# First image's product by channel block while loading, tables copied by ScalarE, second tables and early loads spread over the last image

## Chip, core and metric

The kernel runs on one core of a Trainium2 chip. The metric is device time in microseconds, from one launch to its end. The engines are named as in the profile: PE is TensorE (its weight loads are shown apart as PEld), DVE is VectorE, ACT is ScalarE, POOL is GpSimd, SP is SyncE, which here only issues DMAs. DMAs are issued from SP, ACT and POOL.

## What is computed

The input is a batch of 4 images with 256 channels of 56 x 56 in float32. Four layers follow, each adding its result to its input after a group norm (32 groups of 8 channels):

```
x = x + involution_0(gn(x))     # a 7x7 kernel for each pixel and each of 16 groups of channels
x = x + resblock_1(gn(x))       # two 3x3 convolutions with batch norm, relu, residual
x = x + involution_2(gn(x))     # as layer 0, with batch norms and relu
x = x + gates_3(gn(x))          # a channel gate and a spatial gate

# involution:
h    = reduce_w @ x + reduce_b            # 256 -> 64 channels, at each pixel
kern = span_w @ h + span_b                # 64 -> 16 groups x 49 taps, at each pixel
out[group, c, y, x] = sum over taps of kern[group, tap, y, x] * x[c, y + dy, x + dx]
```

## The kernel before

**Data.** An image is held as two blocks of 128 channels, `[128, 3136]` each. The function `new_block` hands out one of three such buffers. A *unit* is one block of one image, so a layer has eight units. Layers pass images on through DRAM.

**An involution layer** (`involution_layer`, layers 0 and 2). The 56 x 56 pixels are cut into tiles of 3 x 8 (`TY`, `TX`), 19 rows of tiles by 7 columns. `bottleneck` makes `h` for one image: it scales the reducing weights by the norm's factor (L404), multiplies them with the image (L433, at most 9 rows of pixels in one matmul, two row groups side by side in the two halves of the PSUM partitions), evicts with ACT (L450) and copies each half to the other half of the partitions with DVE (L441). The result `hp` is one buffer (`new_h`).

For each unit `tap_matrices` then runs 32 steps. A step multiplies a shifted window of the span weights, `z_sb`, with `hp` (L471) and adds the biases `zb_sb` while evicting: three steps in four by DVE (L489), one by ACT (L482). The result `kt` holds, for each tile, a matrix that takes the 14 x 9 pixels around the tile to the tile's 24 pixels. After each step the functions in `hooks[step]` are called; that is how other work gets its place in the order.

Then come the unit's seven columns of tiles (`apply`): PE multiplies windows `xw` of the image with `kt` (L513), ACT and DVE pick the wanted quarter of each product (L526, L533), and in layer 0 POOL adds it to the image (L538). The windows of a column are made three columns ahead (`NXW`): `next_strip` normalises a strip of the image (POOL, L364), `next_windows` transposes it on PE (L381), ACT copies it out (L382), and four DMAs on SP and POOL shift parts of it within SBUF (L388, L390). Work in `late[column]` follows a column, work in `early[column]` comes before it. `column_sums` takes the statistics for the next layer's norm, and `norm_steps` is a chain of single operations across DVE, PE and POOL that ends in rstd and shift.

**Tables.** `make_tables` builds `z_sb` and `zb_sb` from the span weights: it loads them, copies 16 pieces of 49 elements (L300), two pieces of the biases (L308), makes 24 small matmuls (48 records, L315) and copies the result (L322), with DVE for all copies. In layer 0 it is called once for this layer and once for layer 2; the second result is kept in DRAM until layer 2 begins. The second call is placed in the first unit at steps 3, 14 and 21, and saved at step 22.

**The opening** of layer 0 (L732 to 738): the statistics and norms of both blocks, `bottleneck(0)`, the first tables, `batch_norms`. `since = mark()` comes after these lines (L750): what is written before it is ordered by the planner that places instructions, with its own costs; what follows up to `in_order(since)` keeps on each engine the order in which it is written.

**The convolution layer** (`conv_layer`) transforms rows of the image into six positions (Winograd in the columns, `transform`, L1047 and on) and multiplies them (L1131, L1160, L1242) with weights that were transformed by `row_weights` (L964 to 971). Its first input rows and its first raw weights are loaded ahead by `begin_conv`, which the last unit of layer 0 calls after its first column (`late[0]`, L847). `phases` normalises the rows and sorts them by the four positions; for the first rows ACT does block 0 and DVE block 1 (L1037, L1039). `row_weights` issues its loads from ACT (L952, L953). All eight of these DMAs, four per convolution, carry 384 KB.

Of the kernel before, what the change touches and what calls it, by code (L numbers as in the profile page):

```python
# [16 lines left out]
P = 128  # L17
# [48 lines left out]
def run(g):  # L66
    for _ in g:
        pass
# [3 lines left out]
def net_kernel(  # L72
# [68 lines left out]
    def bn_fold(name, par, gamma, beta, mean, var, n):  # L141

        s = const.tile([P, n], F32, name=f"{name}_s")
        t = const.tile([P, n], F32, name=f"{name}_t")
        rsqrt_eps(s, par(var), BN_EPS)
        nc.vector.tensor_mul(s, s, par(gamma))
        nc.vector.tensor_mul(t, par(mean), s)
        nc.vector.tensor_sub(t, par(beta), t)
        return s, t

# [8 lines left out]
    def batch_norms():  # L159

        par_of = {}
# [8 lines left out]
        s1, t1 = bn_fold("bn1", by_channel, L1_G1, L1_B1, L1_M1, L1_V1, NB)  # L170
        s2, t2 = bn_fold("bn2", by_channel, L1_G2, L1_B2, L1_M2, L1_V2, NB)
        s4, t4 = bn_fold("bn4", by_channel, L2_G, L2_B, L2_M, L2_V, NB)
        s3, t3 = bn_fold("bn3", by_row, L2_G1, L2_B1, L2_M1, L2_V1, 1)

        s4_of = {}
        for n in (2, 4):
            s4_of[n] = const.tile([P, n, NB], F32, name=f"s4_{n}")
            for i in range(n):
                nc.vector.tensor_scalar_mul(s4_of[n][:, i, :], s4, par_of[n][:, i : i + 1])
        bn.update(par=par_of, s1=s1, t1=t1, s2=s2, t2=t2, s3=s3, t3=t3, s4=s4_of, t4=t4)  # L180
# [55 lines left out]
    def load_block(dst, block, parts=1):  # L236
        n = NCHUNK // parts
        for j in range(0, NCHUNK, n):
            at = slice(j * CR * W, min(j + n, NCHUNK) * CR * W)
            nc.sync.dma_start(dst[:, at], block[:, at])  # L240

    def involution_layer(layer, xin, xout, red, span, sb, xs_of, ahead=None, pending=None):

        with ExitStack() as es:
# [12 lines left out]
            def warm(n):  # L257

                ps = one_bank()
                for _ in range(n):  # L260
                    nc.tensor.matmul(ps[:, :P], ident_sb, ident_sb, start=True, stop=True)

            def load(b, cb, parts=1):
                xs_of[b, cb] = new_block()
                load_block(xs_of[b, cb], xin[b][cb], parts)

            for cb in range(NB):
                if (0, cb) not in xs_of:
                    load(0, cb, 3)

            red_sb = wpool.tile([P, NB, 2, R], F32, name="red_sb")
            for i in range(2):
                nc.scalar.dma_start(red_sb[:, :, i], red.rearrange("(cb p) r -> p cb r", p=P))
# [3 lines left out]
            def make_tables(z_sb, zb_sb, span, sb, scratch, eng):  # L277
# [8 lines left out]
                bias_f = scratch[:, n + KK * KK : n + KK * KK + ZN]  # L286
                for i in range(2):
# [4 lines left out]
                nc.gpsimd.memset(z_sb, 0.0)  # L292
                nc.gpsimd.memset(bias_f, 0.0)
                yield
                for i in range(2):
                    half = slice(i * R, (i + 1) * R)
                    for cb in range(NB):
                        m = GB // 2
                        for gp in range(m):
                            nc.vector.tensor_copy(  # L300
                                field(z_sb[half, cb * m + gp, :]),
                                taps[half, cb, :, 2 * gp + i].rearrange("p (y x) -> p y x", x=KK),
                            )


                for i in range(2):
                    half = slice(i * R, i * R + G)
                    nc.vector.tensor_copy(field(bias_f[half]), bias_g[half])  # L308
                yield
                pair = two_banks()  # L310
                for p in range(TP):
                    k, i = divmod(p, 2)
                    half = slice(i * R, i * R + G)
                    z0 = ZF - p // TX * QX - p % TX
                    nc.tensor.matmul(  # L315
                        pair[:Q, i, k * G : (k + 1) * G],
                        bias_f[half, z0 : z0 + Q],
                        ident_sb[half, half],
                        start=True,
                        stop=True,  # L320
                    )
                nc.vector.tensor_copy(  # L322
# [1145 lines left out]
```

## Time and profile before

| | |
|---|---|
| median of 3 runs | 1877.03 us (1874.28 to 1877.57) |
| the profiled execution | 1874.37 us, its span 1872.6 us |
| mean granted PE clock | 0.966 |
| busy share | PE 91%, PEld 81%, DVE 77%, ACT 40%, POOL 23% |
| opening, to the first tap matrix | 36.6 us |
| first unit: tap matrices, columns | 36.0 us, 32.2 us |
| third unit: tap matrices, columns | 24.0 us, 30.3 us |
| last unit of layer 0: tap matrices, columns | 24.0 us, 42.6 us |
| from layer 0's last matmul to the convolution's first | 18 us |

The profile is that of one execution. A line such as `L471 PE MATMUL ps<-hp,z_sb 64*126 64x133 f32` names the line of the kernel, the engine, the operation, and its output and inputs; a matmul in float32 leaves two records. "Busy" is time with an instruction in the engine. A wait names the engine that ended it. The chain of waits follows the work that ended last backwards. SPq, ACTq and POOLq are the queues from which DMAs are issued. In the answers in order of time the columns are start, time, engine, line, operation, and in brackets how long the engine had been idle and what ended that.

### The profile page before, as it was taken

The page shows a single profiled execution, that of the slowest core. Times are in us where ns is not written, and L with a number is a line of the kernel's source. Part 1 is how long each engine was busy: PE and PEld are TensorE (multiplying, and loading weights), DVE is VectorE, ACT ScalarE, POOL GpSimd, SP SyncE. Part 2 cuts the span into 40 slices and gives each one's busy share as a digit, 9 for nine tenths or more (in the row PEclk, how much of TensorE's full clock was granted, in tenths as well). Part 3 has the DMA queues.
Part 4 walks back from the last instruction along what each step waited for, and adds up shares of the span by engine and source line. Part 5 has one row for each costly group of instructions (what it writes and reads, how often), then busy time and mean ns, then how long its engine had stood idle before and what let it go on. Part 6 is the DMA issues. An engine that isn't in the chain of part 4 may idle for free.

```text
span 1872.6 us, 55573 instructions
## 1 busy us (share of the span) xinstructions
PE 1709.5 (91%) x24030; PEld 1509.6 (81%) x24030; DVE 1433.3 (77%) x2823; ACT 748.8 (40%) x1657; POOL 432.2 (23%) x615
## 2 busy tenths in 40 slices
PE   5999999999759999999999999997999898898866
PEld 3888888888748988898899889885877777778865
DVE  5687777876678988898888988865767777777763
ACT  2445445454423222232223212114666565565532
POOL 2323433244210000000000000000000581681672
PEclk9999999999979999999999999998999999999995
DMA  3445544453533111110111210223533764773652
GB/s 97 150 146 177 153 120 140 152 153 111 160 121 100 42 60 61 61 67 36 62 58 57 73 35 33 89 76 89 174 107 132 231 193 147 222 215 105 177 147 76
DMA packets 65589, 215.72 MB, mean 115 GB/s; under 512 B 13564, under 2 KB 20528, under 8 KB 61504
## 3 DMA queue, kind: packets, MB, share of 16 engines
q1 hardware_dynamic: 44448, 141.62, 24.1%
q0 software_dynamic: 14848, 65.85, 10.9%
q10 hardware_dynamic: 6048, 4.68, 0.8%
q8 instruction: 190, 3.11, 0.7%
q14 instruction: 55, 0.45, 0.1%
HBM read 76.24 MB, written 49.16 MB: 67 GB/s over the span
## 4 chain that ended last, share of the span: by engine, by line
PE 65%; DVE 21%; DMA 5%; POOL 3%; issue 3%; ACT 2%; SPq 1%; POOLq 0%; ACTq 0%; DVEq 0%
PE mm L1242 20%; PE ps L513 14%; DVE kt L489 12%; PE mm L1160 10%; PE ps L471 7%; PE mm L1131 6%; PE ps L381 4%; DMA xw<-xw 3%; PE ps L433 2%; DVE un L533 2%; PE ps L700 1%; ACT hp L452 1%; PE ps L596 1%; DVE st L844 1%; DMA xs<-in_x_dram 1%
## 5 line engine op out<-in xcount | busy, mean ns | idle before, releaser
L513 PE MATMUL ps<-kt,xw 126*32 126x48 f32 (+1 forms) x12544 | 383.5, 236 | 56.9 <-DMA xw<-xw 21.3
L513 PEld LDWEIGHTS ps<-kt,xw 126*32 126x32 f32 (+1 forms) x12544 | 344.2, 122 | 102.4 <-issue 48.1
L471 PE MATMUL ps<-hp,z_sb 64*126 64x133 f32 x6144 | 389.0, 282 | 19.2 <-DVE kt L489 7.0
L471 PEld LDWEIGHTS ps<-hp,z_sb 64*126 64x126 f32 x6144 | 370.7, 189 | 34.1 <-DVE kt L489 8.7
L489 DVE TENSOR_TENSOR kt<-ps,zb_sb 126x798 f32<-126x798 f32 x384 | 357.9, 978 | 43.6 <-PE ps L471 43.1
L1242 PE MATMUL mm<-v,u_sb 128*128 128x280 f32 (+1 forms) x1728 | 384.9, 384 | 3.3 <-DVE v L1067 3.3
L1242 PEld LDWEIGHTS mm<-v,u_sb 128*128 128x128 f32 x1728 | 327.6, 190 | 57.8 <-DVE v L1067 3.6
L482 ACT ACTIVATE kt<-ps,zb_sb 126x133 f32<-126x133 f32 x768 | 224.0, 441 | 179.4 <-PE ps L471 179.4
L1160 PE MATMUL mm<-v,u_sb 128*128 128x252 f32 (+1 forms) x936 | 211.2, 386 | 12.6 <-DVE v L1051 12.6
L1160 PEld LDWEIGHTS mm<-v,u_sb 128*128 128x128 f32 x936 | 177.2, 190 | 42.9 <-issue 12.6
L533 DVE SCALAR_TENSOR_TENSOR un<-ps,par_sb,un 128x240 f32<-128x240 f32 x224 | 98.4, 457 | 103.1 <-ACT un L526 98.8
L533 DVE SCALAR_TENSOR_TENSOR un<-ps,s,un 128x240 f32<-128x240 f32 x224 | 102.3, 457 | 92.9 <-ACT un L528 88.7
L1279 POOL DMA_DIRECT2D x<-xs x24 | 13.1, 546 | 684.9 <-DVE xs L1278 539.5
L1227 ACT ACTIVATE res<-xs,shift,norm_sb 128x1120 f32<-128x1120 f32 (+1 forms) x24 | 30.2, 1260 | 235.2 <-DVE xs L1278 119.7
L538 POOL TENSOR_TENSOR xs<-un,xs 128x240 f32<-128x240 f32 x112 | 72.4, 665 | 224.2 <-DVE un L533 224.1
L382 ACT COPY xw<-ps 126x896 f32<-126x896 f32 x112 | 101.5, 907 | 49.6 <-PE ps L381 39.2
L381 PE MATMUL ps<-ident_sb,strip_sb 128*126 128x128 f32 x784 | 111.4, 282 | 1.6 <-DVE kt L489 0.8
L526 ACT ACTIVATE un<-ps,par_sb 128x240 f32<-128x240 f32 x112 | 50.1, 448 | 138.6 <-PE ps L513 136.7
L1131 PE MATMUL mm<-xs,u_sb 128*128 128x126 f32 (+1 forms) x792 | 98.3, 277 | 1.3 <-DVE xs L1094 1.0
L528 ACT ACTIVATE un<-ps,bn_t,s 128x240 f32<-128x240 f32 x112 | 60.1, 538 | 97.8 <-PE ps L513 93.7
L139 POOL TENSOR_TENSOR norm_sb<-norm_sb,mhalf 128x1 f32<-128x1 f32 x32 | 19.2, 602 | 341.7 <-DVE norm_sb L138 341.7
L1131 PEld LDWEIGHTS mm<-xs,u_sb 128*128 128x128 f32 x792 | 94.3, 191 | 2.7 <-issue 1.4
(194 smaller groups left out, 1973.0 us busy)
## 6 DMA issues: line engine op xcount, KB each, us to landing
xw<-xw SPq DMA_DIRECT2D x168, 252.0 KB
xw<-xw SPq DMA_DIRECT2D x224, 126.0 KB
xw<-xw POOLq DMA_DIRECT2D x56, 252.0 KB, 4.7
xs<-x SPq DMA_DIRECT2D x24, 560.0 KB
x<-xs POOLq DMA_DIRECT2D x8, 1568.0 KB, 7.9
xs<-x SPq DMA_DIRECT2D x8, 1568.0 KB
xs<-in_x_dram SPq DMA_DIRECT2D x6, 1568.0 KB
x<-xs SPq DMA_DIRECT2D x6, 1568.0 KB
```

The lines of the kernel that those rows point to most:

```text
L381: nc.tensor.transpose(ps[:Q, k * P : (k + 1) * P], flat[:, k * Q : (k + 1) * Q], ident_sb)
L382: nc.scalar.copy(xw[:, :NSB, :], ps[:Q, : NSB * P].rearrange("q (n c) -> q n c", n=NSB))
L471: nc.tensor.matmul(ps[:Q, i, k * NT : (k + 1) * NT], z_sb[i * R : (i + 1) * R, cb * GB // 2 + gp, z0 : z0 + Q], hp[i * R : (i + 1) * R, py ...
L482: nc.scalar.activation(kt[:, g0 + i, pb, :, k], ps[:Q, i, k * NT : (k + 1) * NT], AF.Identity, bias=zb_sb[:, cb * GB + g0 + i, p0 + k : p0 ...
L489: nc.vector.tensor_tensor(kt[:, g0 : g0 + 2, pb], ps[:Q, :, : PB * NT].rearrange("q i (k t) -> q i t k", k=PB), zb_sb[:, cb * GB + g0 : cb ...
L513: nc.tensor.matmul(v[m * j : m * j + m, i, :, k * TP : (k + 1) * TP], xw[:, window(ty), m * j : m * j + m], kt[:, ng * j : ng * j + ng, :, ...
L528: nc.scalar.activation(part, o[0], AF.Identity, bias=bn["t4"][:, cb : cb + 1], scale=bn["s4"][ng][:, 0, cb : cb + 1])
L533: nc.vector.scalar_tensor_tensor(part, o[e], s, part, ALU.mult, ALU.add)
L538: nc.gpsimd.tensor_tensor(dst, u, dst, ALU.add)
L1131: nc.tensor.matmul(ps[:, co * m : (co + 1) * m], u[ci][:, co * P : (co + 1) * P], v2[:, e, : n // 2, ci * WT : (ci + 1) * WT], start=(ci = ...
L1160: nc.tensor.matmul(ps, u1_sb[:, ci, dy, k, co * P : (co + 1) * P], v[:, k, dy * NB + ci : (dy + n - 1) * NB + ci + 1 : NB, :], start=(j == 0),
L1242: nc.tensor.matmul(ps, u2_sb[:, ci, dy, k, co * P : (co + 1) * P], v[:, k, dy * NB + ci : (dy + n - 1) * NB + ci + 1 : NB, :], start=(j == 0),
```

## The change

In layer 0:

- The first image is loaded in pieces of 4 and 3 chunks (a chunk is eight rows) for block 0 and of 2, 2, 2, 1 for block 1, all from SP. ACT makes one small copy at once. Everything from here on keeps the written order.
- A new function `begin` holds the whole opening. It issues the loads for the first tables and the reducing weights from POOL. The first image's product is no longer made by `bottleneck`: full-width matmuls for block 0 come as soon as its norm is there, and those for block 1 after the second norm. The weights are in both halves, so the copies between the halves are gone. Evictions alternate between ACT and DVE.
- `make_tables` copies with ACT instead of DVE, and yields after every piece; its 24 matmuls can be made in several parts.
- The second tables move from the first unit to the last image: loads at step 16 of the seventh unit, three pieces after each of six of its columns (the last of these is the first of six parts of the matmuls), the other five parts at steps 3 to 18 of the eighth unit, saved at step 22.
- `batch_norms` is a generator whose steps lie between the norms' steps; two of them are at steps 2 and 5 of the first unit.
- The next image's load in the first unit is at step 16 instead of 23.

Between layers 0 and 1:

- `begin_conv` is split. Rows and block 1's raw weights are loaded by SP at step 28 of the eighth unit, block 0's raw weights in three parts by ACT after its first three columns.
- The norm of the last unit's result is no longer run at the end of layer 0, but in steps within the convolutions.
- The weights' loads in `row_weights` are issued by SP, the first rows' phases are all made by ACT and come after the first weight operations, and 28 matmuls of the identity are made before.

```diff
+        for name, par, _, _, _, var, n in folds:
+            bn["s" + name] = const.tile([P, n], F32, name=f"bn{name}_s")
+            bn["t" + name] = const.tile([P, n], F32, name=f"bn{name}_t")
+            rsqrt_eps(bn["s" + name], par(var), BN_EPS)
+        yield
...
+    def load_block(dst, block, parts=(NCHUNK,)):
+        j = 0
+        for n in parts:
+            at = slice(j * CR * W, (j + n) * CR * W)
             nc.sync.dma_start(dst[:, at], block[:, at])
+            j += n
...
+            since = mark()
+            if layer == 0:
+                load(0, 0, (4, 3))
+                load(0, 1, (2, 2, 2, 1))
+
+                nc.scalar.copy(norm_sb[:, 3, B - 1, 1, :], mhalf)
...
+            def load_red():
+                for i in range(2):
+                    eng = nc.gpsimd if layer == 0 else nc.scalar
+                    eng.dma_start(red_sb[:, :, i], red.rearrange("(cb p) r -> p cb r", p=P))
...
-                            nc.vector.tensor_copy(
+                            nc.scalar.copy(
                                 field(z_sb[half, cb * m + gp, :]),
                                 taps[half, cb, :, 2 * gp + i].rearrange("p (y x) -> p y x", x=KK),
                             )
+                            yield
...
+                    nc.scalar.copy(field(bias_f[half]), bias_g[half])
+                yield
+                n = TP // parts
+                zb = zb_sb.rearrange("q g (k i) -> q i k g", i=2)
+                for p0 in range(0, TP, n):
+                    pair = two_banks()
...
+                    nc.scalar.copy(
+                        zb[:, :, p0 // 2 : (p0 + n) // 2],
+                        pair[:Q, :, : n // 2 * G].rearrange("q i (k g) -> q i k g", g=G),
                     )
-                nc.vector.tensor_copy(
-                    zb_sb.rearrange("q g (k i) -> q i k g", i=2),
-                    pair[:Q, :, : TP // 2 * G].rearrange("q i (k g) -> q i k g", g=G),
-                )
-                yield
+                    yield
...
+            def begin():
+
+                steps = lambda g, n: [next(g) for _ in range(n)]
+                tables = make_tables(z_sb, zb_sb, span, sb, new_block(), nc.gpsimd, 1)
+                next(tables)
+                load_red()
+                hp = new_h().rearrange("p (y x a t) -> p y x a t", y=TY, x=TX, t=NTX)
+                nc.gpsimd.memset(strip_sb, 0.0)
+                nc.gpsimd.memset(hp[:, TY - 1, :, NTY - 1, :], 0.0)
+                h_of[0] = hp
+                folds = batch_norms()
+                sums0, sums1 = sums(0, 0), sums(0, 1)
+                redn = work.tile([P, NB, 2, R], F32, name="redn", bufs=1)
+                rstd, shift = norms[0][0]
+                next(folds)
+                steps(tables, 17)
+                warm(8, xs_of[0, 0][:, :P])
+                steps(sums0, NCHUNK)
+                norm = norm_of(0, 0, 0, sums_of[0, 0])
+                steps(norm, 2)
+                next(folds)
+                steps(norm, 1)
+                warm(2, ident_sb)
+                steps(norm, 1)
+                steps(folds, 2)
+                steps(norm, 1)
+                steps(sums1, 2)
+                steps(norm, 1)
+                nc.vector.tensor_scalar_mul(redn[:, 0], red_sb[:, 0], rstd[:, 0:1])
+                steps(sums1, NCHUNK - 2)
+                next(tables)
+                warm(8, ident_sb)
+
+
+                pairs = [two_banks() for _ in range(4)]
+                bank = pairs[3][:, 1, :]
+                norm = norm_steps(sums_of[0, 1], lambda: bank, 0, 0, 1)
+
+                def products(j, ci):
+                    y0 = j * ROWS_H
+                    rows = min(ROWS_H, H - y0)
+                    nc.tensor.matmul(
+                        pairs[j // 2][:, j % 2, : rows * W],
+                        redn[:, ci].rearrange("p i r -> p (i r)"),
+                        xs_of[0, ci][:, y0 * W : (y0 + rows) * W],
+                        start=(ci == 0),
+                        stop=(ci == NB - 1),
+                    )
+
+                for j in range(NH):
+                    products(j, 0)
+                steps(norm, 2)
+                next(folds)
+                steps(norm, 2)
+                next(folds)
+                steps(norm, 2)
+                nc.vector.tensor_scalar_mul(redn[:, 1], red_sb[:, 1], rstd[:, 1:2])
+                for ci in range(NB):
+                    nc.tensor.matmul(
+                        bank[:, 1:2],
+                        red_sb[:, ci].rearrange("p i r -> p (i r)"),
+                        shift[:, ci : ci + 1],
+                        start=(ci == 0),
+                        stop=(ci == NB - 1),
+                    )
+                hb = small.tile([P, 1], F32, name="hb")
+                nc.vector.tensor_add(hb, bank[:, 1:2], by_row(L0_RB))
+                for j in range(NH):
+                    products(j, 1)
+                    rows = min(ROWS_H, H - j * ROWS_H)
+                    a0, n = j * ROWS_H // TY, -(-rows // TY)
+                    s = pairs[j // 2][:, j % 2, : ROWS_H * W].rearrange("p (a y t x) -> p y x a t", y=TY, t=NTX, x=TX)
+                    for py in range(min(rows, TY)):
+                        dst = hp[:, py, :, a0 : a0 + n, :]
+                        if (j + py) % 2 == 0:
+                            nc.scalar.activation(dst, s[:, py, :, :n, :], AF.Identity, bias=hb)
+                        else:
+                            nc.vector.tensor_scalar_add(dst, s[:, py, :, :n, :], hb)
+                return folds
...
-                for cb in range(NB):
-                    run(sums(0, cb))
-                    run(norm_of(0, 0, cb, sums_of[0, cb]))
-                scratch = new_block()
-                run(bottleneck(0))
-                run(make_tables(z_sb, zb_sb, span, sb, scratch, nc.scalar))
-                batch_norms()
-
-                n0 = NB * KK * KK * GB + KK * KK + ZN
-                z2 = scratch[:, n0 : n0 + G // 2 * ZN].rearrange("p (g z) -> p g z", g=G // 2)
-                n0 += G // 2 * ZN
-                zb2 = scratch[:Q, n0 : n0 + G * TP].rearrange("p (g t) -> p g t", g=G)
-                tables2 = make_tables(z2, zb2, span2, sb2, scratch, nc.sync)
-
-                def save():
-                    nc.sync.dma_start(z2_dram, z2)
-                    nc.sync.dma_start(zb2_dram, zb2)
-
-                since = mark()
-                place(hooks0, tables2, (3, 14, 21))
-                hooks0.setdefault(22, []).append(save)
+                place(hooks0, begin(), (2, 5))
...
+            def tables2():
+
+                scratch = room["rows"] = new_block()
+                n0 = NB * KK * KK * GB + KK * KK + ZN
+                z2 = scratch[:, n0 : n0 + G // 2 * ZN].rearrange("p (g z) -> p g z", g=G // 2)
+                n0 += G // 2 * ZN
+                zb2 = scratch[:Q, n0 : n0 + G * TP].rearrange("p (g t) -> p g t", g=G)
+                yield from make_tables(z2, zb2, span2, sb2, scratch, nc.sync, 6)
...
-                    n = (23 if u == 0 else 16) if layer == 0 else (26, 21)[cb]
+                    n = 16 if layer == 0 else (26, 21)[cb]
...
+                last_image = layer == 0 and b == B - 1
+                if last_image and cb == 0:
+                    g2 = tables2()
+                    place(hooks, g2, (16,))
+                elif last_image:
+                    place(hooks, g2, (3, 6, 10, 14, 18, 22, 23))
+                    hooks.setdefault(28, []).append(ahead[0])
...
+                if last_image and cb == 0:
+                    for tx in range(6):
+                        late[tx] += [step(g2)] * 3
+                elif last_image:
+                    for tx in range(3):
+                        late[tx].append(ahead[1 + tx])
...
-            run(norm_of(layer + 1, b, cb, st))
             if layer == 2:
+                run(norm_of(layer + 1, b, cb, st))
...
+    def raw_weights(ci, part, parts, eng):
+        n = 9 * C // parts
+        t = room["h" if ci == 0 else "v2"]
+        w = wc1[ci * P : (ci + 1) * P].rearrange("c k n -> c (k n)")
+        eng.dma_start(t[:, part * n : (part + 1) * n], w[:, part * n : (part + 1) * n])
+
     def begin_conv():
-        room["h"] = new_h()
-        room["rows"] = new_block()
         room["v2"] = new_block()
         load_rows(0, src[1])
-        for ci, t in enumerate((room["h"], room["v2"])):
-            nc.sync.dma_start(
-                t[:, : 9 * C], wc1[ci * P : (ci + 1) * P].rearrange("c k n -> c (k n)")
-            )
-
-    def conv_layer(xin, xout, ahead):
+        raw_weights(1, 0, 1, nc.sync)
+
+    def begin_weights(part):
+        if part == 0:
+            room["h"] = new_h()
+        raw_weights(0, part, 3, nc.scalar)
...
-                    nc.scalar.dma_start(u[:, ci, :, 0, :], w[:, :, 0, :])
-                    nc.scalar.dma_start(u[:, ci, :, 5, :], w[:, :, 2, :])
+                    nc.sync.dma_start(u[:, ci, :, 0, :], w[:, :, 0, :])
+                    nc.sync.dma_start(u[:, ci, :, 5, :], w[:, :, 2, :])
...
-                        if ci == 1 and second is not None:
-                            second.tensor_scalar(dst, xr[:, j], s, t, ALU.mult, ALU.add)
-                        else:
-                            nc.scalar.activation(dst, xr[:, j], AF.Identity, bias=t, scale=s)
+                        nc.scalar.activation(dst, xr[:, j], AF.Identity, bias=t, scale=s)
...
-            g = phases(0, nc.vector)
-            for _ in range(4):
-                next(g)
+            ps = one_bank()
+            for _ in range(28):
+                nc.tensor.matmul(ps[:, :P], ident_sb, ident_sb, start=True, stop=True)
             for _ in range(NB):
                 next(weights1)
-            run(g)
+            run(phases(0))
...
-            tail1, tail2, slow = [], [], []
+
+            tail1, tail2, slow = [], [], [norm_steps(st, one_bank, 1, B - 1, NB - 1)]
...
```

## The prediction

> **What bounds the kernel now.** I read the page first, then busy time by stage, then the chain of waits and the order of events in the stages where TensorE falls short.
>
> ```profile
> span 1872.6 us, 55573 instructions
> ...
> PE 1709.5 (91%) x24030; PEld 1509.6 (81%) x24030; DVE 1433.3 (77%) x2823; ACT 748.8 (40%) x1657; POOL 432.2 (23%) x615
> ```
>
> TensorE (PE) carries the kernel: what can be won lies where it stops or runs slowly. The stages (columns: stretch, length, busy time of PE, PEld, DVE, ACT, POOL, then granted PE clock, DMA share, GB/s):
>
> ```profile
> 36.00:73.00 37.00, 34.16 (x455) 32.60 (x455) 26.38 (x44) 16.66 (x51) 6.14 (x8) 0.85 0.46 141
> ...
> 169.00:194.00 25.00, 24.32 (x392) 23.29 (x390) 24.05 (x35) 14.90 (x49) 3.88 (x6) 1.00 0.46 163
> ...
> 464.00:488.00 24.00, 23.82 (x389) 23.14 (x390) 23.04 (x34) 14.54 (x49) 3.89 (x6) 1.00 0.34 117
> 488.00:531.00 43.00, 29.02 (x812) 25.93 (x812) 15.53 (x35) 10.24 (x20) 12.63 (x19) 0.84 0.55 157
> 531.00:549.00 18.00, 1.46 (x5) 1.30 (x6) 14.85 (x29) 3.37 (x5) 3.43 (x16) 0.61 0.74 241
> ```
>
> The first unit's tap-matrix stage takes 36.0 us (36.57 to 72.56), where the same work takes 24.0 in the third unit (169.13 to 193.10) and the eighth. The eighth unit's columns have 29 us of PE work in 43. After them PE is all but idle for 18. The chain of waits in the opening and the first unit:
>
> ```profile
> 9.36 6.28 DMA xs<-in_x_dram
> ...
> 23.73 7.20 PE ps L433 x26
> 30.93 3.03 PE ps L315 x48
> ...
> 36.57 4.01 PE ps L471 x36
> ...
> 41.49 3.62 PE ps L471 x60
> ...
> 53.08 1.26 DVE xs L300 x8
> ...
> 61.12 2.74 PE ps L315 x48
> ```
>
> The product (L433), the first tables (L315) and the tap matrices (L471) follow each other; then the second tables interrupt the unit (L300, L315). 36 records at the start take longer than 60 later: a cold clock. In order of time around the eighth unit's stall:
>
> ```profile
> 499.27 1.48 SPq L897 DMA_DIRECT2D xs<-in_wc_dram  x1
> ...
> 501.73 0.78 SPq L390 DMA_DIRECT2D xw<-xw  x1
> ...
> 518.27 0.59 PE L513 MATMUL ps<-kt,xw 126*64 126x96 f32 x4 [12.11 <-DMA xw<-xw]
> ```
>
> SP issues the convolution's early loads (3.5 MB) at 497.3 to 500.7; window copies issued behind them land 16 us later and PE stands for 12.1. Where the convolution begins, first the chain, then the order of time:
>
> ```profile
> 537.40 0.82 DVE u_sb L964
> ...
> 543.05 2.81 DVE ph L1037 x4
> ...
> 545.96 0.80 DVE v L1047
> ...
> 548.45 30.35 PE mm L1160 x120
> ```
>
> ```profile
> 537.60 1.08 ACTq L953 DMA_DIRECT2D u_sb<-in_wc_dram  x1
> ...
> 538.73 3.35 ACT L1039 ACTIVATE ph<-xs,norm_sb 128x294 f32<-128x294 f32 x4 [7.71 <-DVE u_sb L964]
> ```
>
> VectorE builds weights, then half of the phases, then the transform; ScalarE issues weight loads until 538.68 before it begins its half.
>
> **The Trainium skill.** (1) "TensorE: Matmul & The Clock Gate", Part 1: an idle array falls to half clock, and about 3.4 us of sustained work restores it. The trace agrees: clock 0.50 from 512 to 524 after the stall, and at 34 to 40. It also drops just after each batch of 48 small table matmuls. (2) "DMA: Bandwidth & Descriptors", Queues, rings and completion order: each DMA engine takes one queue's descriptors in ring order. The window copies landing 16 us after being queued behind loads agree. (3) The same page, Issuing engines are not separate DMA queues: another issuer saves issue time only, the 16 engines being shared. So the weights now issued by ACT still compete with the windows; the trace of before has no such case.
>
> **The change, part by part.** The sum is against the profiled execution: 1874.4 us, of which 1872.6 is span. The median of runs is 1877.0; I subtract the same difference from it.
>
> *Opening, 36.6 us to the first tap matrix: -1.* The loads come in six pieces instead of eight, and the reducing weights, span weights and biases go to POOL's queue (eight issues, at 0.57 us as for L390: 4.6 us, beside memsets, all before its first needed power at about 14). I take 13 us for the last image piece (it was 15.64), but VectorE then sets the pace: 14 statistics at 0.61 = 8.5 us from about 6.8, plus about 2.7 of the first norm, gives 18.5; the second norm's statistics were aggregated at 17.5 before. On PE in written order: first norm until 13.5; 48 table matmuls, 3.0, to 16.5; eight warming matmuls, cold, some 3.7 (estimate: a 133-column matmul pair takes 3.62/15 = 0.24 warm, so 8 x 0.46 cold), to 20.2; seven products of block 0, 5.6 (image 1's 28 warm records took 6.3 for both blocks in half-width pairs, so about 0.9 per full one, the last short), to 25.8. Only now comes the second norm: 4.2 before (17.93 to 22.13), about 3.5 with less VectorE work between, to 29.3. Seven products of block 1, 5.6, and 0.9 for the last evictions: 35.8. The early products are thus not free; they sit ahead of the second norm. What goes is the table step after the product, its 1.09 us copy and six half copies of 0.42. The evictions, 20 over two engines at 0.33, hide under the products; the eighteen table copies on ACT (skill, "ScalarE: Activation LUTs", What ACT_TABLE_LOAD costs: 186 ns + 0.83 N, overlapping by 93, so an estimate of 0.13 to 0.23 for N = 49; VectorE took 0.23; the page's price is a little low, a 133-element one with pointer bias being 391 by it and 441 here) hide under loading. Ends: -4 with a warm clock and early tables, +4 if span weights land 4 us late and the second product runs cold. Batch-norm folding is the same 30 or so 0.15 to 0.3 us operations, in VectorE's gaps.
>
> *First unit: -9.3.* L471 is 384 records at 3.62/60 = 23.2 us; three extra windows at 0.91 are 2.7; start and end 0.8 as in the third unit: 26.7, against 36.0. Gone are 2.7 of L315, about 3.6 of cold clock, and waits for VectorE's 18 copies. VectorE has 24 L489 at 0.99 = 23.8 and under 2 of folding, so it stays just covered. Ends: -10 to -7.5 (cold start). The next image's load moves from hook 23 to 16, where later units have it.
>
> *Second tables in the last image: +4.7.* Unit seven: 16 ACT copies, three per column (0.4 to 0.75 us), fit in the 1.27 us that ACT idles after each window copy; without that cover they would delay the column's first scaling, at most 0.75 each. But in its sixth column PE reaches the first table part right after the window transposes, while ACT still has a 0.91 window copy and three table copies: about 1.8 of PE wait plus 0.5 of work. Everything on PE is queued behind it. Five parts in unit eight's tap stage cost 40 records at 0.057 = 2.3, which nothing hides since PE is busy 23.8 of 24. Their PSUM copies add perhaps 0.3 each to ACT, idle 9 us there. SP gets six small loads at hook 16, POOL two memsets; neither has urgent work then. Ends: +2.5 to +6.
>
> *Early loads: -8.5 in unit eight.* Row and block-1 weight loads (2.4 MB) leave SP at hook 28, near 485. At the stall's 270 to 330 GB/s they land near 494, when the first window copies are due; they may wait for the 0.8 MB table save issued at hook 22, 4 us ahead. Then 393 KB goes out on ACT after each of three columns. The floor is five columns of 4.1 and three of 3.2, 29.9 from 489.3; it took 41.1, so 11.2 is the most. Windows have only some 7 us between their copy and their use, and unit seven, with no loads at all, took 32.3. Windows move about 0.77 MB per column (189 GB/s); with the weights 285. I leave 2.8 of lateness. Ends: -11.2 to -2. ACT pays three issues of about 0.6.
>
> *Convolution's start: -5.5.* The last norm (4 us of small steps, ending in POOL's 536.14 power, before which POOL would not clear the borders) moves into the convolution. VectorE is free at 533.5: scales 0.3, six weight operations 5.65, memset 0.2, three transform steps 2.35: PE starts at 542.1. ACT needs 8 x 0.84 = 6.7 for all phases, no longer behind its 4 us of issuing; starting at 533.8 it ends at 540.5, so PE starts near 543.0 instead of 548.45. Weight loads move to SP, where the next rows wait for the phases anyhow. 28 warming matmuls (6 us) lie in PE's idle time and may save 1.5 of cold clock; the postponed norm adds about 1 to VectorE later. Ends: 0, if ACT must wait for VectorE's memset after the weights, to -7.5.
>
> Sum: -1 - 9.3 + 4.7 - 8.5 - 5.5 = -19.6. Profiled 1854.8; **median 1857**. The third layer does the same work in the same order.
>
> **Rivals.** *Collision moved.* Weights and windows share the DMA engines, and unit eight wins 2 instead of 8.5: 1864. For: windows arrive just in time. Against: two thirds of the bytes now leave before the columns. *Long opening.* POOL's issues bring the tables late, PE's order adds 4 more and the products run cold, +7 in all: 1864. For: the norm queued behind seven products. Against: the loads can end 2 us sooner. *ACT stuck behind its loads (slower).* An ACT issue waits for an earlier DMA, as SP's did at 4.88 for another queue's load; every scaling, then VectorE and PE stand behind it. Three such waits of 12.1, as long as PE's was, are 36.3: 1894. It decides from 23.4/3 = 7.8 us each. Against: the big loads should have landed before the first. *No change:* every part at its upper end is +4 - 7.5 + 6 - 2 + 0 = +0.5: 1877.5.
>
> **How the numbers follow.** A measurement of this kernel can tell about 0.2% (3.8 us) from no change. Likeliest 0.66, collision 0.13, long opening 0.10 (all faster, 0.89), no change 0.04, slower 0.07. The likeliest's range is 1848 to 1863: best ends in two parts, worst in one or two. With the first two rivals and their upper ends, 1847 to 1868; about a tenth lies above, as much below.
>
> **What would show it.** First tap matrix near 35.8, and PE's second norm behind the first seven products; the first tap stage 27 us at full clock; a PE wait of near 2 us in unit seven's sixth column; unit eight's tap stage near 26.3 and its columns near 33; PE's gap before the convolution 12 to 13 us. The prediction is wrong if windows still land late by more than 5 us, if ACT shows waits at its weight issues, or if its phases begin only after VectorE's weights.

## The result and the profile after

The changed kernel takes 1877.44 us (median of 12 runs, 1871.75 to 1890.12). The kernel before takes 1876.37 us on the same chip (12 runs, 1868.18 to 1880.96). The ratio is 1.0008, with a 95% interval from 0.9991 to 1.0025: no difference that can be measured. The prediction of 1857 (1847 to 1868) was wrong. The profiled execution took 1880.72 us, of which 1878.9 is span. The head of its page, with the busy time of each engine:

```profile
span 1878.9 us, 55768 instructions
...
PE 1736.5 (92%) x24122; PEld 1527.8 (81%) x24122; DVE 1420.7 (76%) x2785; ACT 759.3 (40%) x1695; POOL 437.6 (23%) x623
```

TensorE is busy for 27 us more than before, and 18 of these lie in the opening: 33.30 us in 125 records, where the opening of before had 15.37 us in 89. Busy time by stage, with the columns as in the prediction:

```profile
0.00:54.70 54.70, 33.30 (x125) 21.85 (x125) 15.86 (x58) 10.11 (x31) 12.21 (x26) 0.72 0.23 71
54.70:80.40 25.70, 25.70 (x405) 24.68 (x406) 22.48 (x32) 16.06 (x50) 4.74 (x6) 1.00 0.48 155
...
473.43:500.71 27.28, 26.93 (x429) 25.71 (x429) 23.07 (x32) 15.32 (x53) 3.42 (x6) 1.00 0.57 202
500.71:533.53 32.82, 28.77 (x814) 25.56 (x812) 15.34 (x33) 9.95 (x19) 12.84 (x19) 0.95 0.50 139
533.53:545.48 11.95, 6.52 (x57) 6.36 (x57) 10.90 (x19) 7.15 (x9) 2.92 (x15) 1.00 0.68 238
```

The rows are the opening, the first unit's tap matrices, the eighth unit's tap matrices, the eighth unit's columns and the stretch up to the convolution's first matmul. The first row is the surprise: 54.70 us, against 36.57 before. Each later row is near what was predicted. The table gives TensorE's stage lengths from both traces, each from the first matmul of one kind to the first of the next.

| stage | before | after | difference | predicted |
|---|---|---|---|---|
| opening, to the first tap matrix | 36.57 | 54.70 | +18.1 | -1 |
| first unit, tap matrices | 35.99 | 25.70 | -10.3 | -9.3 |
| first unit's columns | 32.17 | 32.26 | +0.1 | 0 |
| units two to six, and seven's tap matrices | 326.00 | 325.07 | -0.9 | 0 |
| unit seven, columns | 33.18 | 35.70 | +2.5 | +2.4 |
| unit eight, tap matrices | 23.97 | 27.28 | +3.3 | +2.3 |
| unit eight, columns | 42.56 | 32.82 | -9.7 | -8.5 |
| then to the convolution's first matmul | 18.01 | 11.95 | -6.1 | -5.5 |
| convolution's first matmul at | 548.45 | 545.48 | -3.0 | -19.6 |

The predicted column splits the prediction's +4.7 for the second tables into 2.4 for unit seven and 2.3 for unit eight.

What is left of the gain at that point, 3.0 us, does not show in the medians. In the ten profiles of this study, the time from the convolution's first matmul to the end of the span runs from 1312.9 to 1340.2 us. The kernel before has 1324.1 of it, the changed kernel 1333.4, and no edit of the experiments touches work behind that point. The convolution layer accounts for little of it: from its first matmul to the third layer's first tap matrix it is 739.4 us in the kernel before, 740.4 in the changed one, and at most 744.0 in the ten. The rest is the third layer, 584.7 and 593.1 in these two, and 573.1 to 596.2 in the ten. Why was not settled. So a single execution can't show a few microseconds in the total, and the experiments that were timed once are read from their stages. Their totals, in the order of the text, are 1865.5, 1869.5, 1879.3, 1880.1 and 1883.0 us.

Here is the order of time on the changed kernel, first the opening and then the places that the prediction named:

```profile
12.37 0.31 DVE L138 TENSOR_SCALAR bn_s<-cp 128x2 f32<-128x2 f32 x3 [12.37 <-DMA cp<-in_cpar_dram]
...
14.22 3.77 DVE L358 BATCH_NORM_STATS2 st<-xs 128x6 f32<-128x448 f32 x7
...
20.37 5.30 PE L340 MATMUL ps<-ident_sb,xs 16*126 16x16 f32 x48
...
29.18 6.52 PE L527 MATMUL ps<-xs,redn 128*128 128x504 f32 x14
...
38.88 2.05 PE L527 MATMUL ps<-xs,redn 128*128 128x504 f32 x2 [0.22 <-DVE hb L552]
...
42.28 3.73 PE L527 MATMUL ps<-xs,redn 128*128 128x504 f32 x4 [1.36 <-ACT hp L561]
...
47.37 3.73 PE L527 MATMUL ps<-xs,redn 128*128 128x504 f32 x4 [1.36 <-ACT hp L561]
...
54.70 2.32 PE L577 MATMUL ps<-hp,z_sb 64*126 64x133 f32 x36 [0.91 <-ACT hp L561]
...
466.85 0.86 PE L340 MATMUL ps<-ident_sb,xs 16*126 16x16 f32 x8 [1.58 <-ACT xs L330]
...
506.42 0.35 ACTq L1007 DMA_DIRECT2D hp<-in_wc_dram  x1
...
535.93 6.72 ACT L1154 ACTIVATE ph<-xs,norm_sb 128x294 f32<-128x294 f32 x8 [1.86 <-POOL xs L644]
...
545.48 6.88 PE L1275 MATMUL mm<-v,u_sb 128*128 128x280 f32 x21 [4.01 <-DVE v L1166]
```

And the same places in the kernel before, again in order of time:

```profile
6.13 0.31 DVE L138 TENSOR_SCALAR bn_s<-cp 128x2 f32<-128x2 f32 x3 [4.09 <-DMA cp<-in_cpar_dram]
...
6.35 1.15 DVE L333 BATCH_NORM_STATS2 st<-xs 128x6 f32<-128x448 f32 x2
...
30.86 3.08 PE L315 MATMUL ps<-ident_sb,xs 16*126 16x16 f32 x48
```

The reader should see three things. In both kernels VectorE's first work on loaded data is an addition for a batch-norm factor, which waits for its parameters (`cp`), and statistics stand behind it. Before, `cp` is there at 6.13 us and statistics begin at 6.35; now it is there at 12.37, the addition that needs `rp` comes ahead of the statistics too, and they begin at 14.22. The 48 table matmuls take 5.30 us where they took 3.08. And the products of the second block, from 38.88 on, come in pieces with stops of 1.36 us: 15.8 us until the first tap matrix, for fourteen records.

The chain of waits of the changed kernel begins with the parameters as well, with `rp`, the last of them to land:

```profile
2.26 11.79 DMA rp<-in_rpar_dram
...
14.31 3.70 DVE st L358 x7
```

### The profile page after: what moved, and what is told of

It reads as the page before. It is cut to its first block, busy times and chain, and to the rows that moved or that the text cites. A ratio compares the mean times of both kernels' runs of the same rounds, so it can differ in the third digit from the quotient of the medians.

```text
span 1878.9 us, 55768 instructions
## 1 busy us (share of the span) xinstructions
PE 1736.5 (92%) x24122; PEld 1527.8 (81%) x24122; DVE 1420.7 (76%) x2785; ACT 759.3 (40%) x1695; POOL 437.6 (23%) x623
## 4 chain that ended last, share of the span: by engine, by line
PE 69%; DVE 19%; issue 4%; POOL 3%; DMA 2%; ACT 2%; SPq 0%; ACTq 0%; POOLq 0%; DVEq 0%
PE mm L1357 20%; PE ps L619 16%; DVE kt L595 11%; PE mm L1275 10%; PE ps L577 8%; PE mm L1246 5%; PE ps L407 4%; PE ps L459 2%; DVE un L639 1%; PE ps L806 1%; DMA xw<-xw 1%; PE ps L702 1%; DMA rp<-in_rpar_dram 1%; ACT hp L478 1%; PE ps L527 1%
## 5 line engine op out<-in xcount | busy, mean ns | idle before, releaser
L619 PE MATMUL ps<-kt,xw 126*32 126x48 f32 (+1 forms) x12544 | 387.5, 237 | 35.3 <-DVE kt L595 16.0
L577 PE MATMUL ps<-hp,z_sb 64*126 64x133 f32 x6144 | 385.0, 280 | 15.9 <-DVE kt L595 4.4
L577 PEld LDWEIGHTS ps<-hp,z_sb 64*126 64x126 f32 x6144 | 366.3, 187 | 30.7 <-issue 6.2
L407 PEld LDWEIGHTS ps<-ident_sb,strip_sb 128*126 128x126 f32 x784 | 83.9, 140 | 20.1 <-issue 10.1
```

What stands on the lines that cost most here:

```text
L407: nc.tensor.transpose(ps[:Q, k * P : (k + 1) * P], flat[:, k * Q : (k + 1) * Q], ident_sb)
L577: nc.tensor.matmul(ps[:Q, i, k * NT : (k + 1) * NT], z_sb[i * R : (i + 1) * R, cb * GB // 2 + gp, z0 : z0 + Q], hp[i * R : (i + 1) * R, py ...
L619: nc.tensor.matmul(v[m * j : m * j + m, i, :, k * TP : (k + 1) * TP], xw[:, window(ty), m * j : m * j + m], kt[:, ng * j : ng * j + ng, :, ...
```

## The experiments

The theory after the traces has two causes of about equal size. (A) The batch-norm powers stand ahead of the statistics on VectorE, and their small parameter transfers land late among the image pieces. (C) A product waits for the eviction of the one before it where the two share a tile of two banks, though each has its own bank, and each eviction passes from ScalarE to VectorE and back. The rivals are named with each run.

**The batch-norm factors after the statistics.** The first `next(folds)` and those within the first block's norm go; all four steps follow the second block's statistics.

```diff
-                next(folds)
                 steps(tables, 17)
...
                 steps(sums1, NCHUNK - 2)
+                steps(folds, 4)
                 next(tables)
```

> The changed kernel with one move: the batch-norm powers and the folding steps after them come after the second block's statistics, so that VectorE's first operation is a statistic of block 0 and not an addition that needs the parameter loads. Theory A (VectorE stood 7.4 us for the parameters, and everything behind it shifted): statistics start near 6.7 instead of 14.2, first tap matrix near 47.5 instead of 54.7. Theory B (the opening is paced by TensorE's order and clock, VectorE's wait is covered): first tap matrix stays above 53.

Measured: the statistics start at 6.78, the first tap matrix comes at 46.74 instead of 54.70, 8.0 us earlier, and the convolution's first matmul at 537.28 instead of 545.48. (A) holds, with its size. From this trace in order of time, the second block's products:

```profile
31.85 1.11 PE L523 MATMUL ps<-xs,redn 128*128 128x504 f32 x2 [0.39 <-DVE hb L548]
34.32 3.73 PE L523 MATMUL ps<-xs,redn 128*128 128x504 f32 x4 [1.36 <-ACT hp L557]
39.42 3.73 PE L523 MATMUL ps<-xs,redn 128*128 128x504 f32 x4 [1.36 <-ACT hp L557]
```

They stop as before, and still take 14.9 us (31.85 to 46.74). The two causes are separate.

**The second block's products in another order.** Neighbouring products no longer share a tile.

```diff
-                for j in range(NH):
+                for j in (0, 2, 4, 6, 1, 3, 5):
                     products(j, 1)
```

> The changed kernel with the second block's products in the order 0, 2, 4, 6, 1, 3, 5, so that two neighbours never share a two-bank tile. Theory C (a product waits for the eviction of the other bank of its tile): TensorE runs the seven products in about 6.5 us without a stop, and the stage from its first product to the first tap matrix falls from 15.8 us to between 8.5 and 10 (evictions still pass from one engine to the other, 20 at 0.43 = 8.6). Theory D (the evictions' hand-over between ScalarE and VectorE alone sets the pace): 15 or more.

Measured: all fourteen records without a stop, in the order of time of this kernel:

```profile
37.42 7.25 PE L527 MATMUL ps<-xs,redn 128*128 128x504 f32 x14 [0.39 <-DVE hb L552]
```

The stage takes 8.66 us (37.42 to 46.08) instead of 15.8. The work is the same and only the order differs. Of the 7.2 us, 4.1 are the three stops and 3.6 are the products themselves, whose records take 7.25 us instead of 10.8; 0.5 goes back in a longer wait at the end. The granted clock was 0.80 over this stage, and 0.59 over the same stage of the changed kernel. Here too it stood at 0.51 from 38.9 to 42.3 us, with no stop, so the stops do not begin the low clock. Whether they make it last longer is taken up in the fourth experiment.

**Each product evicted by one engine.** The condition `(j + py) % 2 == 0` becomes `j % 2 == 0`. The three evictions of a product no longer change hands, but the order of the products stays.

> The changed kernel with all evictions of one product on one engine (even products ScalarE, odd ones VectorE), order unchanged. Theory C: TensorE still stops after every pair, but each eviction group costs three back-to-back operations: the stage falls from 15.8 us by 2 to 4, since two groups can now run side by side. Theory D: the stage falls to 8 or less.

Measured: the stage takes 15.6 us (38.42 to 54.01) instead of 15.8. In order of time:

```profile
41.55 3.73 PE L527 MATMUL ps<-xs,redn 128*128 128x504 f32 x4 [1.08 <-ACT hp L561]
46.35 3.73 PE L527 MATMUL ps<-xs,redn 128*128 128x504 f32 x4 [1.08 <-ACT hp L561]
51.16 2.45 PE L527 MATMUL ps<-xs,redn 128*128 128x504 f32 x4 [1.08 <-ACT hp L561]
```

Each of the three stops shrinks only from 1.36 to 1.08 us, and the wait at the end from 0.91 to 0.40: 1.35 us in all. One engine does its three evictions in 0.99 us, where the two in turn took 1.27 (40.96 to 42.23 in the changed kernel). The last group of four records, which took 1.32 us in the changed kernel, takes 2.45 here, which loses 1.13 of it again: the clock was 1.00 there and is 0.50 here, and why is not shown. The hand-over between the engines is thus not the cause of the stops; the wait for the eviction of the tile's other bank is. The gain falls short of the expected 2 to 4 us. Two eviction groups do not run side by side, since the products come one at a time (VectorE's second group ends at 44.6, ScalarE's begins at 45.31).

**The parameters' transfers first.** SyncE issues `cp` and `rp` ahead of the image, instead of ScalarE beside it.

```diff
-    nc.scalar.dma_start(cp, cpar.rearrange("(cb p) n -> p cb n", p=P))
+    nc.sync.dma_start(cp, cpar.rearrange("(cb p) n -> p cb n", p=P))
...
-        nc.scalar.dma_start(rp[i * R : (i + 1) * R, :], rpar)
+        nc.sync.dma_start(rp[i * R : (i + 1) * R, :], rpar)
```

> The changed kernel with the parameter loads (cp, rp) issued by SP ahead of the image loads instead of by ACT beside them. Theory A1 (they are late because image pieces issued at the same time crowd them out): parameters land near 5, statistics start near 7 to 8, first tap matrix near 48. Rival A2 (the small pieces of 52 and 20 bytes are slow in themselves): they land after 10 as before, and the opening stays near 54.

Measured, in order of time:

```profile
2.83 3.17 DVE L138 TENSOR_SCALAR bn_s<-cp 128x2 f32<-128x2 f32 x3 [2.83 <-DMA cp<-in_cpar_dram]
...
10.74 3.85 DVE L358 BATCH_NORM_STATS2 st<-xs 128x6 f32<-128x448 f32 x7 [4.74 <-DMA xs<-in_x_dram]
```

The 13 KB of parameters, which landed at 12.37 us in the changed kernel, are there at 2.83 us when nothing is ahead of them, so small pieces are not slow in themselves. But statistics miss the expected 7 to 8 us, since the image's first piece is now the late one: issued 1.8 us later, it lets them begin only at 10.74. The first tap matrix comes at 45.85, 8.9 us earlier than in the changed kernel and about as early as with the factors moved, but for a mixed reason: 3.5 us from the statistics, 3.0 from the second block's products (12.8 us instead of 15.8), and 2.3 from the steps between, where the table matmuls took 3.98 us instead of 5.30. The second block's stops are the same three of 1.36 us, yet the granted clock is 0.87 over the stage, not 0.59. Stops of this length alone do not keep the clock low.

What makes the parameters late shows in the packets that the queues moved. In the changed kernel ScalarE's queue moves 50 to 65 packets in each microsecond from 3 to 6, beside an image queue that moves 0.34 to 0.39 MB in each; POOL's queue moves its first packets only after 5. In the kernel before SyncE stands until 4.88 us before it issues more of the image; from 5 to 6.1 us the image queue moves only 0.09 MB (0.39 in the changed kernel), and ScalarE's queue 821 packets (54). POOL's span weights, which are the other new load in the changed kernel, may add to the delay after that; no run has them out of the way.

**The old opening, all else as changed.** Sums, norms, product and first tables are issued as in the kernel before, with the tables' copies on VectorE and the planner ordering the whole; the other parts of the change stay.

```diff
...
-                place(hooks0, begin(), (2, 5))
+                for cb in range(NB):
+                    run(sums(0, cb))
+                    run(norm_of(0, 0, cb, sums_of[0, cb]))
+                scratch = new_block()
+                run(bottleneck(0))
+                run(make_tables(z_sb, zb_sb, span, sb, scratch, nc.scalar, 1, nc.vector))
+                run(batch_norms())
+                since = mark()
```

> The changed kernel with the opening of the kernel before (sums, norms, first image's product and first tables by VectorE, in that order, placed by the planner); all the rest of the change stays. Theory A (the opening alone ate the gain; the parts at units seven and eight and the convolution's start are worth what their stages show, about 21 us): first tap matrix at 36.6, first unit's tap matrices back near 36 us, so the first unit ends some 8 us earlier than in the changed kernel (54.7 + 25.8 = 80.5 against 36.6 + 36.1 = 72.7), the convolution's first matmul near 537.5, and the total about 8 us under the changed kernel, near 1869, a ratio of 0.996 to the kernel before. Theory B (the later gains are lost again in the convolution and the third layer): the first matmul of the convolution near 537.5 all the same, but a total within 0.2% of the kernel before, 1873 to 1880.

Measured: 1855.15 us (1850.78 to 1861.41, 6 runs), a ratio of 0.9874 [0.9846, 0.9903] to the kernel before. First tap matrix at 36.24, the convolution's first matmul at 529.27. The expectation put the first unit's tap matrices back at 36 us, which was wrong. They take 27.13 (36.24 to 63.37), against 25.70 in the changed kernel, so all but 1.4 us of their gain belongs to what left that unit, the second tables above all, as the prediction had it, and not to the new opening. The 8.9 us by which this stage is shorter than expected also account for the convolution's start, 8.2 us earlier than expected. The total is 14 us below the expected 1869; the 6 us that this leaves lie behind the convolution's start and are not explained. With that, theory A of this run is confirmed and its rival is not: everything but the opening brings about 21 us in the medians (19.2 at the convolution's first matmul), and the convolution and third layer do not take it back.

**Three edits to the new opening.** Factors after the statistics, products in the other order, and one engine for each tile of products.

```diff
-                        if (j + py) % 2 == 0:
+                        if j in (0, 4, 1, 5):
```

> The changed kernel with three edits to its opening: the batch-norm powers after the statistics, the second-block products in the order 0, 2, 4, 6, 1, 3, 5, and both evictions of a product by one engine, ScalarE for products 0, 4, 1, 5 and VectorE for the others, so that the engines work side by side. Theory A with C: statistics from 6.8, first-block products at 23.2, second-block products at 31.85 without a stop and at most 7.3 us, evictions 1.0 us a product on two engines, first tap matrix at 38 to 39.5; the first unit's tap matrices stay at 26; the convolution's first matmul 15.5 to 17 us earlier than in the changed kernel, at 529 to 530; total about 1861 (1857 to 1866), a ratio of 0.992 to the kernel before. Theory B (later layers give it back): total within 0.2% of the kernel before.

Measured: 1863.7 us (1857.27 to 1870.47, 6 runs), a ratio of 0.9922 [0.9893, 0.9951]; first tap matrix at 39.68, the convolution's first matmul at 530.30, 15.2 us before the changed kernel's. The total is inside the expected range; the first tap matrix and the convolution's start miss theirs by 0.2 and 0.3 us. The second block's stage takes 7.75 us, 0.9 less than with the order alone.

**And without the second warming.** The eight warming matmuls ahead of the first block's products go.

```diff
                 next(tables)
-                warm(8, ident_sb)
```

> As the one with the three edits to the opening, and without the eight warming matmuls ahead of the first-block products (3.7 us of TensorE's time from 19.65 on, in the run with the powers put later). If they buy no clock (the first-block products took 5.44 us, 0.39 a record, right behind them): products start near 19.8, the second norm's matmuls follow at 25.2 instead of 28.4, and the first tap matrix comes 2.5 to 3.7 us earlier than in that kernel. If they do buy clock: products slower by as much, first tap matrix the same to 1 us.

Measured: 1852.96 us (1841.55 to 1855.94, 6 runs), a ratio of 0.9856 [0.9825, 0.9887]. From the order of time of the kernel with the three edits, and then of this one:

```profile
19.96 3.49 PE L272 MATMUL ps<-ident_sb 128*128 128x128 f32 x16
...
23.29 5.44 PE L523 MATMUL ps<-xs,redn 128*128 128x504 f32 x14
```

```profile
19.07 7.50 PE L522 MATMUL ps<-xs,redn 128*128 128x504 f32 x14
```

The warming does make the products behind it faster: it takes 3.49 us and saves 2.06. The first tap matrix comes at 37.53 instead of 39.68, 2.2 us earlier, which lies between the two expectations (2.5 to 3.7, and within 1). The medians are 11 us apart, and every run of this kernel is below every run of that one, but the convolution's first matmul (526.88) comes only 3.4 us earlier. In the two profiles, which are 17.7 us apart, the third layer makes up 14.6. With six runs each and no overlap, this is hardly scatter between executions alone; what sets the third layer's time stays open. This is the fastest of the kernels tried, though it can't be told apart from the one with the old opening (their intervals overlap).

**The early loads in one place.** All of the convolution's early loads are again issued by SyncE after unit eight's first column.

```diff
-                    hooks.setdefault(28, []).append(ahead[0])
...
-                    for tx in range(3):
-                        late[tx].append(ahead[1 + tx])
+                    late[0] += ahead
...
-        raw_weights(0, part, 3, nc.scalar)
+        raw_weights(0, part, 3, nc.sync)
```

> The changed kernel with the convolution's early loads all issued by SyncE in one place again, after the first column of unit eight, instead of one there and three by ScalarE a column apart. If the spreading is what shortened unit eight's columns (42.56 to 32.82 us): the windows transfers wait behind the loads again and the columns take 40 to 43 us, the convolution's first matmul comes 7 to 10 us later than in the changed kernel. If the shortening came from elsewhere in the change (the tables gone from this unit's columns, or the normalization put off): the columns stay within 2 us of 32.8.

Measured: unit eight's columns take 43.85 us (32.82 in the changed kernel), and the convolution's first matmul comes at 557.30, 11.8 us later. The list of waits for these columns, with total, times and longest:

```profile
PE ps L619 <- DMA xw<-xw: 8.7, 1, 8.7
...
PE ps L619 <- issue: 4.1, 2, 3.7
```

The wait for windows is back. The spreading alone is worth what was seen (9.7 us), and both figures lie slightly above what was expected.

## Why the prediction was wrong

*Opening (-1; measured +18.1).* This is the step that failed. Its 35.8 us became 54.70, 18.9 more, and the traces split that up:

- "VectorE then sets the pace: 14 statistics ... from about 6.8": +7.4. They began at 14.22. The prediction called the folding "the same 30 or so" operations "in VectorE's gaps", and so put VectorE's wait for their parameters at nothing. Their first operations stand ahead of the statistics, and VectorE stands until the parameters land. That was so before as well, but ended at 6.13, and VectorE had to wait for the image's later pieces anyway (until 13.90). The prediction listed what ScalarE's queue lost to POOL's, but not when `cp` and `rp`, still in ScalarE's queue, would land beside image pieces that are now larger and issued with shorter pauses. Moving the factors confirmed it (8.0 us).
- "Seven products of block 1, 5.6, and 0.9 for the last evictions": +9.3. The stage took 15.82. "The evictions, 20 over two engines at 0.33, hide under the products" is the sentence that fell. Two products share one tile of two banks, so in order the second waits for the first's evictions, three of 0.4 us one after the other. The products also ran at a clock of 0.59 on average. Another order of the products took 7.2 us of it away.
- "48 table matmuls, 3.0": +2.3, taking 5.30 at a clock of 0.50. The row of before (3.08) stood behind the products, where TensorE had been busy; here it follows small norm steps. The seven first products took 6.4 instead of 5.6, +0.8, at a mean clock of 0.83, since they too began at half clock.
- The second norm behind the seven products, 3.5, was right: 3.3 (35.54 to 38.88). First norm and warming were 0.8 shorter than predicted together.

*First unit (-9.3; measured -10.3), second tables (+4.7; +5.8), early loads (-8.5; -9.7) and the convolution's start (-5.5; -6.1)* were right, in mechanism and, to about 1 us each, in size. The wait in unit seven's sixth column is 1.58 us before the first table part. ScalarE's three weight issues take 0.35 each and nothing waits behind them, so the rival in which ScalarE gets stuck did not occur. Its phases ended at 542.65 and did not wait for VectorE's weights. The runs with the old opening and with the loads in one place confirm two of these directly: without the new opening the kernel takes 1855 us, inside the predicted range, and loads in one place cost 11.0 us in unit eight's columns.

*The rivals.* The time hit was that of "no change", 1877.5, but not by its account, in which every part came out at its upper end. The true case was "long opening", with its doubt about cold products in the right place but its size at +7 instead of +18; its other reasons, late tables and the norm queued behind seven products, added nothing to the predicted sum. The bounds of the opening, -4 to +4, allowed for the clock and for late span weights. They were too narrow because no bound was put on when the operand of VectorE's first instruction lands, nor on what frees a tile.

## What to carry to other kernels

When a stage is rewritten in an order of its own, go through each engine's first instruction and ask when its operand lands, and through each tile written twice and ask whose reading frees it: durations of single instructions don't tell either. Small work ahead of large work costs little as long as its operands land early, as they did here before the loads were changed; when they land late, everything on its engine stands behind it. A net gain of 21 us was hidden by a loss of 18 in one place, so time the parts alone before judging the whole.

## What the runs showed of the hardware

- A 13 KB transfer issued at 1.17 us, beside 3.2 MB of image pieces in another queue, landed at 12.37 us, 11 us after its issue. Issued first, at 0.73, it landed at 2.83. In the kernel before it was also beside the image, but landed at 6.13: its queue moved 821 packets from 5 to 6.1 us, while the image queue ran low, and 54 in the same time in the changed kernel.
- Small matmuls did not bring the clock back. In the changed kernel TensorE had work without a visible wait from 18.43 to 35.54 us. The 48 table matmuls of 16 columns ran their whole 5.30 us at a clock of 0.50, the warming behind them (3.51 us) too, and the mean over the 14 product records that followed was 0.83. In the kernel with the three edits, warming in front of such 14 records took 3.49 us and saved 2.06, against the same kernel without it.
- Stops of 1.36 us between groups of four records did not settle the clock. In the changed kernel two groups of 3.73 us ran at 0.50 and the last, which has fewer columns, at 1.00 (1.32 us). With the parameters first and the same stops, the second group took 1.96 us at 1.00. What ends the low clock is not shown.
